# Pool adds up softmax numerators of three key tiles before TensorE sums them

## The chip, the cores and the metric

The kernel runs on one core of a Trainium2 chip. Its engines work side by side, each through its own queue of instructions in order: TensorE (PE in the profile; its weight loads are listed as PEld), VectorE (DVE), ScalarE (ACT), GpSimd (POOL) and SyncE (SP), whose queue here holds most of the DMA issues. An instruction starts when it is at the head of its engine's queue and when the semaphores that it waits for have come. The metric is the time of one execution on the device in microseconds (us); the time before is the median of three runs.

## The reference, cut to what matters

The reference is a decoder of two layers on an input of 4 batches x 512 tokens x 512 features, with layer norms behind each part: causal self-attention, cross-attention and a feed-forward part in layer 0; causal self-attention, a mixing of tokens by a thresholded similarity and a mixture of experts in layer 1. The change concerns the two self-attentions:

```python
    def _L0_attn_ref(hidden_states, Wq, bq, Wk, bk, Wv, bv, Wo, bo):
        HIDDEN = 512
        NUM_HEADS = 16
        ...
        scores = jnp.einsum('bhqd,bhkd->bhqk', q, k) * scale
        causal = jnp.tril(jnp.ones((S, S), dtype=bool))
        scores = jnp.where(causal, scores, jnp.float32(-jnp.inf))
        attn = jax.nn.softmax(scores, axis=-1)
        out = jnp.einsum('bhqk,bhkd->bhqd', attn, v)
```

and, because of tiles that share a buffer, the mixing part, whose thresholds depend only on the second input `ctx_512` and are worked out ahead, beside the self-attentions:

```python
    def _L1_xattn_ref(h, adj_raw, Wq, Wk, gamma_raw):
        ...
        sim = jnp.einsum('bhnd,bhmd->bnm', Q, K) / (jnp.sqrt(jnp.float32(d)) * H)
        k = max(1, int(n * TOP_K_RATIO))
        topk_vals = jax.lax.top_k(sim, k)[0]
        threshold = topk_vals[:, :, -1:]
```

## The kernel before, in words

The stages follow one another in time: self-attention of layer 0 (0 to 540 us), cross-attention (540 to about 1010), feed-forward (to 1414), self-attention of layer 1 (1414 to 1945), mixing and routing (to 2190), experts (to 2584).

**A self-attention** treats 16 groups `n`, each 4 heads of one batch (`n = 4 b + g`). Keys lie on the partitions and queries along the free dimension, so scores are held transposed. Per group there are four key tiles `kb` of 128 keys; by causality tile `kb` needs only the queries from 128 `kb` on, so its numerators `p0` to `p3` are 4 heads x 512, 384, 256 and 128 queries, float32. The steps of one group are: `maxima` (L228–249: scores with queries on partitions, DVE takes each query's greatest score), `parts` (L251–259: DVE splits the maxima into three bfloat16 parts), `least` (L261–269: PE transposes them, ACT copies the result to `nmT`), `softmax(n, kb)` (L273–296: PE computes the transposed scores with the negated maxima and the causal mask added, ACT takes the exponential in two instructions of two heads each, which makes `p0` to `p3`), `values` (L298–315) and `finish` (DVE: reciprocal and product).

`values(n)` runs two passes of matmuls over the same numerators: with weights `ones` it sums the numerators over the keys (into a PSUM tile of the `tp` pool), with weights `va` it makes the weighted values (into a tile of the `mm` pool). In both, each key tile and each head is one matmul, 16 per pass, and the profile shows every such float32 matmul as two records. After each pass ACT copies the result out (L311).

The order of the work is written out by hand: a loop over time steps `t` with `n, m = divmod(t, 4)` issues, at each step, `maxima(n, 3 - m)`; `least(n - 1)` at `m = 0`; `values(n - 2)` at `m = 1` or else a projection of the next batch; one `softmax` call of group `(t - 5) // 4`, with `kb` in the order 2, 1, 0, 3; then `finish`, `parts` and one step of a background generator. `in_order` (L416–429) chains PE's matmuls of the self-attention in that order. On the other engines a scheduler places the instructions; each engine keeps the order it got. The last batch of each layer has no next batch's projections beside it. PSUM pools in this stage: three pairs (`sc`), one `tp` buffer, one `mm` buffer.

**The background** of layer 0 is `split_context` (L435–461) followed by the threshold selection of batches 0 and 1; that of layer 1 is the selection of batches 2 and 3. `split_context` loads a 128 x 512 tile `ct` of the context per batch, scales it on Pool and splits it there into three bfloat16 parts `ct0`, `ct1`, `ct2`, which SP writes to DRAM (`ctx_part`); behind the four batches come 12 DMAs from `ctx_part` to `keys` and 16 from a tile of ones to `keys`, for the cross-attention. The selection loads the same context tile again (`scT`, L950–951, in `Similarities.tile`), makes two projections `sqk` and four similarity tiles `sim` with six matmuls per batch (L955, L960), each through the one `tp` buffer and a copy out, and then bisects for the threshold (L992–1010): in each step ACT takes signs with a running count (L998, into the tag `junk`, two buffers), and Pool updates `mid` with five small operations (L1006–1010). Two halves of two tiles take turns. At the end of a bisection ACT and DVE use a tile `y` (L1018–1021).

All tiles of the background come from one pool (`sims` in layer 0, `sims2` in layer 1) with one buffer per tag where nothing else is said: tiles of one tag share its buffers and wait for each other.

Of the kernel before, what the change touches and what calls it, by code (L numbers as in the profile page):

```python
# [13 lines left out]
F32 = mybir.dt.float32  # L14
BF16 = mybir.dt.bfloat16
U32 = mybir.dt.uint32
AF = mybir.ActivationFunctionType
ALU = mybir.AluOpType
# [3 lines left out]
P = 128  # L22
B, S, D = 4, 512, 512
NT = S // P
# [16 lines left out]
def decoder_kernel(ctx: ExitStack, tc: tile.TileContext, a: dict, out: bass.AP):  # L41
    nc = tc.nc
    V, A, G, T = nc.vector, nc.scalar, nc.gpsimd, nc.tensor
# [17 lines left out]
    def psum_tp(dt=F32, n=4):  # L61
        return ps["tp"].tile([P, n, P], dt, tag="tp", name="tp")

    def psum_mm():
        return ps["mm"].tile([P, 512], F32, tag="mm", name="mm")
# [10 lines left out]
    ones = const.tile([P, P], F32, tag="ones", name="ones")  # L76
# [59 lines left out]
    def self_attention(pre, first, background=lambda: None):  # L136
        HD, NG, NJ = 32, 4, 4
        scale = 1.0 / math.sqrt(HD)
        multiply, transpose = in_order()
        with tc.tile_pool(name=pre + "w", bufs=1) as wp, tc.tile_pool(  # L140
            name=pre + "qkv", bufs=2
# [126 lines left out]
                NM[n] = po.tile([P, S], BF16, tag="nmT", name="nmT")  # L268
                A.copy(NM[n], tp.rearrange("p i t -> p (i t)"))

            PR = {}

            def softmax(n, kb):  # L273

# [2 lines left out]
                m = S - kb * P  # L277
                p = PR[n, kb] = po.tile(
                    [P, NJ, m], F32, tag=f"p{kb}", name=f"p{kb}", bufs=2 if kb == 2 else 1
# [14 lines left out]
                for h in range(NJ // 2):  # L294
                    heads = p[:, 2 * h : 2 * h + 2, :]
                    A.activation(heads, sc[h][:, :, :m], AF.Exp)  # L296

            def values(n):  # L298

                b, g = divmod(n, NG)  # L300
                o, t = psum_mm(), psum_tp().rearrange("p n t -> p (n t)")
                for to, left in ((t, None), (o, VA[b % 2])):
                    for kb in range(NT):
                        for j in range(NJ):
                            multiply(
                                to[HD * j : HD * (j + 1), kb * P :],
                                ones[:, :HD] if left is None else left[:, kb, NJ * g + j, :],
                                PR[n, kb][:, j, :], start=(kb == 0), stop=(kb == NT - 1),
                            )
                    u = po.tile([P, S], F32, tag="us" if left is None else "u", name="u", bufs=1)  # L310
                    A.copy(u, to)  # L311
                    if left is None:
                        sums = u
                        yield
                if g == 0:
                    O[b] = po.tile([P, NG, S], F32, tag="oT", name="oT", bufs=1)
                F[n] = sums, u
# [59 lines left out]
            for t in range(NT * total + 6):  # L377
                n, m = divmod(t, NT)
                k = t - 5
# [14 lines left out]
                if m == 1 and n > 1:  # L394
                    dense = values(n - 2)
                elif t >= 6:
                    dense = project(b, u // NT, "qkv"[u % NT]) if b < B and u % NT < 3 else iter(())
                else:
                    dense = begin(2)
# [35 lines left out]
    def split_context(pool):  # L435


        for b in range(B):
            ct = pool.tile([P, S], F32, tag="ct", name="ct")
            nc.sync.dma_start(ct, a["ctxT"][:, ts(b, S)])  # L440
            G.tensor_scalar(ct, ct, 0.25, None, ALU.mult)
            for k in range(3):
                c = pool.tile([P, S], BF16, tag=f"ct{k}", name=f"ct{k}")
                G.tensor_copy(c, ct)
                nc.sync.dma_start(ctx_parts[k][:, ts(b, S)], c)
                if k < 2:
                    G.tensor_tensor(ct, ct, c, ALU.subtract)
            yield
        for p, k in enumerate(KPART):
            nc.sync.dma_start(  # L450
                keys[0][ts(p, XD)], ctx_parts[k].rearrange("(g d) t -> d g t", d=XD)
            )
        one = pool.tile([P, S], BF16, tag="ct0", name="ct0")
        G.memset(one, 1.0)
        for r in range(P // 32):
            nc.sync.dma_start(
                keys[1][32 * r : 32 * r + XD], ctx_parts[2].rearrange("(g d) t -> d g t", d=XD)
            )
            for b in range(B):
                nc.sync.dma_start(  # L460
                    keys[1][32 * r + XD : 32 * (r + 1), :, ts(b, S)],
                    one[:XD].unsqueeze(1).to_broadcast([XD, XG, S]),
                )
        yield
# [472 lines left out]
    class Similarities:  # L937
# [8 lines left out]
        def tile(self, b, i, tag="sim"):  # L946

            if self.b != b:
                self.b = b
                cT = self.pool.tile([P, S], F32, tag="scT", name="scT")  # L950
                nc.sync.dma_start(cT, a["ctxT"][:, ts(b, S)])
                self.qk = []
                for k in range(2):
                    ps = psum_tp().rearrange("p n t -> p (n t)")
                    T.matmul(ps, self.w[k], cT, start=True, stop=True)  # L955
                    t = self.pool.tile([P, S], F32, tag=f"sqk{k}", name=f"sqk{k}")
                    V.tensor_copy(t, ps)
                    self.qk.append(t)
            ps = psum_tp().rearrange("p n t -> p (n t)")
            T.matmul(ps, self.qk[0][:, ts(i, P)], self.qk[1], start=True, stop=True)  # L960
            s = self.pool.tile([P, S], F32, tag=tag, name=tag)
            A.activation(s, ps, AF.Copy, scale=float(np.float32(1.0 / (math.sqrt(32.0) * 4))))
            return s
# [432 lines left out]
    with tc.tile_pool(name="sims", bufs=1) as mp:  # L1396
        selection, background = selecting((0, 1), mp, split_context(mp))
        with psum(3, 1, 1):
            self_attention("L0", True, background)
            for _ in selection:  # L1400
                pass
# [17 lines left out]
    with tc.tile_pool(name="sims2", bufs=1) as mp:  # L1419
        selection, background = selecting((2, 3), mp)  # L1420
        with psum(3, 1, 1):
            self_attention("L1", False, background)
            for _ in selection:
                pass
# [49 lines left out]
```

## Time and profile before

| what | value |
|---|---|
| runs | 2602.18, 2584.24, 2590.51 us; median 2590.51 us |
| profiled execution | 2586.26 us; span of its core 2584.5 us |
| mean granted PE clock | 0.956 |
| PE busy, 0–540 us / 1414–1945 us | 484.17 of 540 / 483.29 of 531 us |
| ACT busy, same stretches | 208.50 / 220.53 us |
| DVE busy, same stretches | 269.23 / 265.57 us |
| POOL busy, same stretches | 100.72 / 70.01 us |
| granted PE clock, same stretches | 0.97 / 0.95 |
| first block of `sums` records, 512 columns (by shape) | 256 records, 35.6 us |
| 384, 256, 128 columns | 27.0, 19.9, 13.0 us |

Line 1 of the page gives each engine's busy time and its share of the span. The slices cut the span into 40 equal parts of 64.6 us; each digit is a busy share in tenths. A row of the groups names source line, engine, operation, the tiles written and read, partitions x elements, and the count; behind the first bar stand total busy time and mean duration in ns, behind the second the idle time of the engine just before, and what ended it. The timeline lists start, duration, engine, line and tiles; an engine with a trailing q is its queue of DMA issues, and a bracket gives the idle time before and what ended it. PE's records overlap since matmuls are pipelined, so the length of a pass is read from the start of the first matmul to the start of the work behind it.

### The profile page before, as it was taken

What the parts mean: (1) busy time and instruction counts of PE and PEld (TensorE: products, weight loads), DVE (VectorE), ACT (ScalarE), POOL (GpSimd) and SP (SyncE); (2) the same over time, 40 slices, a digit from 0 to 9 for tenths busy, and PEclk for the clock granted to TensorE, in tenths of its full rate; (3) what the DMA queues carried; (4) which work ended last, traced back from release to release, by engine and by line L of the source; (5) the groups of instructions that cost most, each with busy time, mean ns of one, the idle gap of its engine ahead of it and who ended that gap; (6) DMA issues with size and microseconds to landing.
All of it is one profiled execution on the core that took longest, in us unless ns stands there. A gap on an engine that the chain in (4) does not pass through costs nothing. (4 is left out here: it accounts for less than half of the span.)

```text
span 2584.5 us, 34904 instructions
## 1 busy us (share of the span) xinstructions
PE 2284.4 (88%) x13080; PEld 1010.3 (39%) x13080; DVE 1437.7 (56%) x3146; ACT 1128.1 (44%) x1770; POOL 624.9 (24%) x1218
## 2 busy tenths in 40 slices
PE   6899999979899899998995899989985999999995
PEld 2334333423333333355553334434342334444442
DVE  2455455567878788578886355545554672111117
ACT  0632462326777677656663443282331430221211
POOL 7300120033334233066674310040000004000004
PEclk9999999889999999999998999989987999999997
DMA  6500000072412210000001100000001006534535
GB/s 217 149 22 1 1 1 1 1 265 94 130 34 91 74 34 17 1 1 1 1 1 32 52 1 1 1 1 1 1 3 58 9 1 231 164 106 157 173 118 183
DMA packets 89884, 156.93 MB, mean 61 GB/s; under 512 B 7152, under 2 KB 39280, under 8 KB 89712
## 3 DMA queue, kind: packets, MB, share of 16 engines
q1 hardware_dynamic: 72304, 115.86, 13.9%
q10 hardware_dynamic: 12288, 22.03, 2.3%
q0 software_dynamic: 5120, 16.78, 2.0%
q8 instruction: 103, 1.69, 0.3%
q14 instruction: 69, 0.57, 0.1%
HBM read 161.99 MB, written 47.71 MB: 81 GB/s over the span
## 5 line engine op out<-in xcount | busy, mean ns | idle before, releaser
L552 DVE TENSOR_REDUCE nm<-sc 128x2 f32<-128x1024 f32 x256 | 304.2, 1218 | 99.7 <-PE sc L422 99.1
L590 ACT ACTIVATE p<-sc 128x1024 f32<-128x1024 f32 x256 | 248.5, 1024 | 135.3 <-PE sc L422 135.3
L246 DVE CUSTOM_DVE_ANT_0 e<-sc,late_keys 128x256 bf16<-128x256 f32 (+3 forms) x512 | 222.8, 484 | 130.9 <-PE sc L422 130.7
L296 ACT ACTIVATE p<-sc 128x512 f32<-128x512 f32 (+3 forms) x256 | 165.9, 700 | 234.1 <-PE sc L422 233.9
L422 PE MATMUL mm<-p,va 128*32 128x512 f32 (+3 forms) x2048 | 217.4, 529 | 0.4 <-ACT oT L605 0.3
L1339 PE MATMUL sc<-wug,xbT 128*128 128x512 f32 x384 | 185.9, 600 | 12.8 <-issue 7.0
L422 PE MATMUL sc<-qs,ks 128*128 128x512 bf16 x512 | 149.7, 384 | 29.3 <-DVE nm L552 28.1
L422 PE MATMUL sc<-ks,qs 128*128 128x512 bf16 x512 | 158.3, 394 | 1.8 <-DVE nm L552 1.6
L422 PE MATMUL sc<-kT,qT 32*128 32x512 f32 (+3 forms) x1024 | 128.8, 497 | 19.1 <-ACT p L296 15.7
L324 DVE RECIPROCAL u<-u 128x128 f32<-128x128 f32 x128 | 108.4, 909 | 64.6 <-ACT u L311 64.6
L422 PE MATMUL sc<-qT,kT 32*128 32x256 f32 (+3 forms) x1024 | 129.2, 504 | 14.4 <-DVE st L246 12.5
L998 ACT ACTIVATE junk<-sim,mid 128x512 bf16<-128x512 f32 x176 | 125.1, 724 | 16.3 <-POOL mid L991 16.3
L1366 POOL DMA_INDIRECT yg<-ys,pi x32 | 33.4, 1043 | 364.3 <-DMA ys<-yb 340.4
L743 POOL TENSOR_TENSOR y<-z 128x512 f32<-128x512 f32 (+1 forms) x48 | 97.4, 2041 | 87.3 <-DVE z L728 87.3
L1346 DVE TENSOR_TENSOR h<-sc,sl 128x256 f32<-128x256 f32 x48 | 20.2, 421 | 163.4 <-ACT sl L1344 163.4
L1339 PEld LDWEIGHTS sc<-wug,xbT 128*128 128x128 f32 x384 | 68.5, 192 | 82.4 <-issue 74.9
L743 POOL TENSOR_TENSOR z<-y 128x512 f32<-128x512 f32 x64 | 95.2, 1506 | 3.4 <-issue 2.1
L1353 PE MATMUL sc<-wd,hT 128*128 128x512 f32 x192 | 93.2, 609 | 0.0
L422 PEld LDWEIGHTS sc<-kT,qT 32*128 32x128 f32 x1024 | 49.7, 188 | 109.5 <-issue 74.1
L422 PEld LDWEIGHTS <-ks 128*128 128x128 bf16 x512 | 50.2, 99 | 108.1 <-issue 63.1
L1336 DVE COPY xbT<-tp 128x512 f32<-128x512 f32 x48 | 32.9, 685 | 104.6 <-PE tp L1334 104.6
L422 PEld LDWEIGHTS sc<-qT,kT 32*128 32x128 f32 x1024 | 50.4, 191 | 92.0 <-issue 62.0
(299 smaller groups left out, 4255.5 us busy)
## 6 DMA issues: line engine op xcount, KB each, us to landing
wug<-in_Wu SPq DMA_DIRECT2D x48, 512.0 KB
wug<-in_Wg SPq DMA_DIRECT2D x48, 512.0 KB
wd<-in_Wd SPq DMA_DIRECT2D x48, 512.0 KB
xs<-zero SPq DMA_DIRECT2D x3, 4096.0 KB
xb<-xs SPq DMA_DIRECT2D x48, 256.0 KB
ys<-yb ACTq DMA_DIRECT2D x48, 256.0 KB
w<-in_w_gate SPq DMA_DIRECT2D x16, 512.0 KB
w<-in_w_up SPq DMA_DIRECT2D x16, 512.0 KB
```

The costliest lines, as they stand in the source:

```text
L246: V.tensor_tensor_reduce(e, at[r], late_keys[:, (NT - m) * P :], 1.0, LOWEST, ALU.add, ALU.max, accum_out=st[:, i, r : r + 1],)
L296: A.activation(heads, sc[h][:, :, :m], AF.Exp)
L324: V.reciprocal(sums[:, ts(i, P)], sums[:, ts(i, P)])
L422: ins = op(*args, **kw)
L552: V.tensor_reduce(NM[n][:, i, 2 * h : 2 * h + 2], sc, AX.X, ALU.max, negate=True)
L590: A.activation(p[:, 2 * h : 2 * h + 2, :], sc[h], AF.Exp)
L743: then(pool, getattr(G, op)(*args))
L998: A.activation(e, s[k], AF.Sign, bias=bias[:, k : k + 1], accum_out=to[:, k : k + 1])
L1336: V.tensor_copy(xbT, tp)
L1339: T.matmul(pp[:, 0, :], xbT[:, c, :], wug[s][:, c, :, :].rearrange("p q f -> p (q f)"), start=(c == 0), stop=(c == NK - 1),)
L1353: T.matmul(pp[:, 1, :], hT[:, c, :], wd[s][:, c, :], start=(c == 0), stop=(c == F // P - 1),)
L1366: G.indirect_dma_start(out=y, out_offset=None, in_=ys, in_offset=bass.IndirectOffsetOnAxis(pos[k][:, t : t + 1], 0),)
```

## The change

In `softmax`, Pool adds the numerators that several key tiles have for the same later queries. A new tile `R[n]` (tag `r`, 4 heads x 384 queries, float32, one buffer) stands for queries 128 to 511. With `kb == 1`, `R`'s last 256 columns become `p1 + p2`; with `kb == 0`, its first 128 columns become `p1 + p0` and `p0` is added to its last 256. Each is done for two heads at a time, six Pool instructions per group. In `values`, the pass with `ones` now sums `p0`'s first 128 columns, `R` and `p3`, 12 matmuls in place of 16; the pass with `va` is as it was. The remaining edits are tags: `ct` and `scT` take the tag `y` (one buffer), `ct0` to `ct2` the tag `junk` (two buffers), where each had a buffer of its own.

```diff
-            PR = {}
+            PR, R = {}, {}
...
                     A.activation(heads, sc[h][:, :, :m], AF.Exp)
 
+                for h in range(NJ // 2):
+                    heads = slice(2 * h, 2 * h + 2)
+                    if kb == 1:
+                        if not h:
+                            R[n] = po.tile([P, NJ, S - P], F32, tag="r", name="r", bufs=1)
+                        G.tensor_tensor(
+                            R[n][:, heads, P:], p[:, heads, P:], PR[n, 2][:, heads, :], ALU.add
+                        )
+                    elif kb == 0:
+                        r = R[n][:, heads, :]
+                        G.tensor_tensor(
+                            r[:, :, :P], PR[n, 1][:, heads, :P], p[:, heads, P : 2 * P], ALU.add
+                        )
+                        G.tensor_tensor(r[:, :, P:], r[:, :, P:], p[:, heads, 2 * P :], ALU.add)
+
             def values(n):
...
                 for to, left in ((t, None), (o, VA[b % 2])):
-                    for kb in range(NT):
+
+                    if left is None:
+                        parts = [(PR[n, 0][:, :, :P], 0), (R.pop(n), 1), (PR[n, 3], 3)]
+                    else:
+                        parts = [(PR[n, kb], kb) for kb in range(NT)]
+                    for p, q in parts:
                         for j in range(NJ):
                             multiply(
-                                to[HD * j : HD * (j + 1), kb * P :],
-                                ones[:, :HD] if left is None else left[:, kb, NJ * g + j, :],
-                                PR[n, kb][:, j, :], start=(kb == 0), stop=(kb == NT - 1),
+                                to[HD * j : HD * (j + 1), q * P : q * P + p.shape[2]],
+                                ones[:, :HD] if left is None else left[:, q, NJ * g + j, :],
+                                p[:, j, :],
+                                start=q < (2 if left is None else 1),
+                                stop=q == NT - 1 or (left is None and q == 0),
                             )
...
-            ct = pool.tile([P, S], F32, tag="ct", name="ct")
+            ct = pool.tile([P, S], F32, tag="y", name="ct")
...
-                c = pool.tile([P, S], BF16, tag=f"ct{k}", name=f"ct{k}")
+                c = pool.tile([P, S], BF16, tag="junk", name=f"ct{k}", bufs=2)
...
-        one = pool.tile([P, S], BF16, tag="ct0", name="ct0")
+        one = pool.tile([P, S], BF16, tag="junk", name="ct0", bufs=2)
...
-                cT = self.pool.tile([P, S], F32, tag="scT", name="scT")
+                cT = self.pool.tile([P, S], F32, tag="y", name="scT")
```

## The prediction

> **What bounds the kernel now.** I read the page's busy line and its slices first.
>
> ```profile
> PE 2284.4 (88%) x13080; PEld 1010.3 (39%) x13080; DVE 1437.7 (56%) x3146; ACT 1128.1 (44%) x1770; POOL 624.9 (24%) x1218
> ...
> PE   6899999979899899998995899989985999999995
> ...
> POOL 7300120033334233066674310040000004000004
> ```
>
> TensorE (PE) is busy 88% of the span and Pool 24%; in the slices of the two self-attentions (0–540 us, 1414–1945 us) PE shows 9s where Pool shows 0 to 3. The averages hide stages with different limits, so next the busy times of single stretches (columns: window, length, busy and count of PE, PEld, DVE, ACT, POOL, granted clock, DMA share, GB/s):
>
> ```profile
> 195.00:260.00 65.00, 64.88 (x429) 27.28 (x428) 34.69 (x111) 18.40 (x28) 0.00 (x0) 1.00 0.00 1
> 1615.00:1680.00 65.00, 64.54 (x426) 26.77 (x423) 36.80 (x109) 19.11 (x29) 0.24 (x2) 1.00 0.00 1
> 82.00:141.00 59.00, 50.55 (x309) 19.94 (x308) 29.13 (x91) 49.55 (x122) 23.52 (x125) 0.91 0.33 79
> 1679.00:1743.00 64.00, 52.18 (x352) 21.64 (x348) 29.73 (x80) 51.78 (x128) 28.98 (x132) 0.89 0.00 1
> 540.00:544.00 4.00, 1.04 (x8) 0.88 (x9) 1.96 (x4) 0.61 (x1) 4.00 (x9) 0.51 1.04 327
> 544.00:548.00 4.00, 3.30 (x14) 1.54 (x14) 1.59 (x2) 1.41 (x2) 3.29 (x9) 0.50 1.06 405
> 548.00:552.00 4.00, 3.93 (x26) 2.22 (x24) 4.00 (x4) 1.11 (x2) 3.08 (x8) 0.71 1.05 410
> ```
>
> Rows 1 and 2: in the plain stretches PE never waits and Pool is free, so work taken off PE is time saved. Rows 3 and 4, beside the selection of batches 0 and 3: ScalarE (ACT) is the busier engine for its part, 49.55 of 59 and 51.78 of 64 us; PE waits some 15% there. Rows 5 to 7: after PE stood still (7.5 us from 534 to 542) its granted clock is 0.51, 0.50, then 0.71. Idle time of PE costs more than itself.
>
> **Part 1: fewer columns in the sums.** The timeline of one group in a plain stretch, and of the last two groups of L0 (columns: start, duration, what, count):
>
> ```profile
> 221.66 2.36 PE L422 MATMUL tp<-p,ones 128*32 128x512 f32 x32
> 223.95 0.71 PE L422 MATMUL sc<-qT,kT 32*128 32x256 f32 x8
> 241.37 1.94 ACT L296 ACTIVATE p<-sc 128x1024 f32<-128x1024 f32 x2 [3.43 <-PE sc L422]
> ...
> 498.92 1.94 ACT L296 ACTIVATE p<-sc 128x1024 f32<-128x1024 f32 x2 [2.98 <-PE sc L422]
> 501.38 2.36 PE L422 MATMUL tp<-p,ones 128*32 128x512 f32 x32 [0.52 <-ACT nmT L269]
> 510.98 2.60 ACT L296 ACTIVATE p<-sc 128x1024 f32<-128x1024 f32 x4 [1.01 <-PE sc L422]
> 512.86 2.35 PE L422 MATMUL tp<-p,ones 128*32 128x512 f32 x30
> ```
>
> The sums pass holds PE from 221.66 to 223.95, 2.29 us for 512+384+256+128 = 1280 columns per head. After the change it has 128+384+128 = 640. By columns that is 1.15 us; small blocks cost more than their share (0.22–0.27 us for 128 columns against 0.86 for 512), so I take 1.2–1.25 left and a gain of 1.05 us (0.9 to 1.15). There are 32 groups, 16 per layer; 28 of them are dense: 28 × 1.05 = **−29.4** (−25 to −32).
>
> **Part 2: Pool's adds.** Per group two of 2x256 elements per partition (for `kb`=1), then two of 2x128 and two of 2x256 (for `kb`=0): 192 instructions. The groups that price them (mean ns after the bar's first number):
>
> ```profile
> L193 POOL TENSOR_TENSOR x<-x,L0bo 128x512 f32<-128x512 f32 x16 | 19.7, 1265 | 0.0
> L618 POOL TENSOR_TENSOR x<-oc,x 128x256 f32<-128x256 f32 x32 | 26.2, 820 | 108.5 <-DVE oc L614 108.5
> ```
>
> So 2 × 1.265 = 2.5 us for `kb`=1 and 2 × (0.82+1.265) = 4.2 us for `kb`=0; from the first half's exponential to a finished `R` 3.9 to 4.6 us, since the second half follows without a gap. In the dense group above the first half ends at 242.34, `R` at about 247; the next sums pass of that group stands at some 250.7. The cover is 3.7 us of other matmuls: cost nothing. If it were gone, each group would lose what `R` is late.
>
> Cover is missing in the last two groups of each layer, with no projections left. n=14: exponentials from 498.92 (half ends about 499.9), `R` at 503.9–504.5, sums at 501.38 now; the 128 columns of `p0` run meanwhile, 384 and 128 columns (0.64 + 0.25) behind `R`, so it ends at 504.8–505.4 where it ends at 503.7 now: +1.1 to +1.7. n=15: half ends 512.0, `R` 516–516.6, sums end 516.9–517.5 where they end at 515.2 now: +1.7 to +2.3. Two layers: **+6.5** (5.6 to 8).
>
> What DVE pays: at 54.03 a DVE instruction with two SBUF operands, `rest` (L255), took 1.18 us beside Pool's L193 adds, at 205.00 alone 0.18; the PSUM-fed maxima don't stretch. `parts` has four such, up to 3 us later, needed some 4 us after: 0 (bound +3). The Trainium skill ("GPSIMD Engine Reference", Engine selection) speaks against putting a two-input elementwise operation on GpSimd, about twice as slow as VectorE. Rows here agree (1.265 us, against 0.69 for 512-wide DVE operations at L325), and by that rule the adds on DVE would shorten `R`'s chain by half, at most the 6.5 of the tail.
>
> **Part 3: the tags, at the beginning of L0.** `ct2` now shares two buffers with `ct0` and `ct1`, and `scT` shares one with `ct`. So batch 0's `scT` load (L951), issued at 27.51, can't start before the last `ct` is dead, and in SP's queue it now stands behind all the split's DMAs. In the order of instructions on each engine it goes from position 13 to 54, where the third `xt` load stands now. And PE's six similarity matmuls of batch 0 stand in a row behind `maxima(1,3)`, ahead of `least(1)`. The queue and PE now:
>
> ```profile
> 27.51 0.45 SPq L951 DMA_DIRECT2D scT<-in_ctxT  x1
> 65.23 6.00 SPq L450 DMA_DIRECT2D keys<-ctx_part  x8
> ...
> 97.64 0.61 SPq L181 DMA_DIRECT2D xt<-in_xT  x1
> ...
> 66.79 1.02 PE L955 MATMUL tp<-scT,swq 128*128 128x512 f32 x2
> 96.01 0.40 PE L422 MATMUL tp<-ident,pm 128*128 128x128 bf16 x4
> ```
>
> PE reaches that place at about 96.0 − 6.3 (the similarity matmuls and their waits, no longer before it) − 2.0 (an exponential's wait that goes) = 88. The load can be issued at 97.64 at the earliest; the keys' transfers drain at about 100.3, so its 256 KB land at about 101.5; the split itself is later by δ: each `ct2` cast waits for `ct0`'s write (about 3 us), and the next `ct` for it, hence δ = 4.6 (1 to 8). The load lands at 106, PE stands 18 us (14 to 22). The order in PE's queue is fixed, so the ready scores and values of group 0 stand behind it. Then six matmuls with one PSUM buffer go in turn with their copies: 1.8 us each by 66.79 to 68.54, 10.8 against 5.7 now, +5 (4 to 6). Then the clock: +4 (0 to 8) by the rows at 540–552, half speed for some 8 us. **+27** (18 to 36). The Trainium skill ("TensorE: Matmul & The Clock Gate", Part 1) has full speed back after about 3.4 us of sustained work; by it the clock would cost at most 2. The rows at 544–552, busy 3.30 and 3.93 of 4 us and still at 0.50 and 0.71, say longer.
>
> In L1 and for later loads `scT` is wanted over 100 us after its buffer is free: nothing.
>
> **Part 4: Pool's adds in the selection.** A bisection step is ACT's signs, then five small Pool operations of 0.2 us (1.2 us for the chain), then the next signs; two halves alternate, so one half's two signs (1.45 us) cover the other's Pool work. In the changed order about eight blocks of adds (2.5 or 4.2 us) stand among these steps. Each holds ACT for 1.05 or 2.75 us, about 15 in all, and exponentials and `nmT` copies stand behind the signs. Half of it reaching PE: **+8**; nothing if ACT catches up, 20 if all does and the clock falls with it.
>
> **Sum.** −29.4 + 6.5 + 27 + 8 = +12. The profiled execution took 2586.26 us (span 2584.5, 1.8 around it): **2598**. That execution lies 4 under the median, 2590.51, so by the median it would be 2602. All good bounds: −32+6+18 = −8; all bad: −25+8+3+36+20 = +42.
>
> **Rivals.**
> - B: the load isn't late at PE, because PE gets there later than 88 or the load is issued past the keys' DMAs. Only the serial chain stays: −29.4+6.5+5+8 = −10: 2576 (2566 to 2582). For it: nothing but the shared buffer orders the load. Against: position 54 in SP's queue.
> - C, slower: Pool in the selection. Where a block of adds outlasts the 1.45 us of the other half's signs, ACT waits, PE waits behind its exponentials, and the clock falls: eight blocks lose their whole 3.35 us, 27, and some 5 at low clock in place of +8: 2622 (2613 to 2633). It decides as soon as PE has no ready matmuls ahead. For it: ACT at 81–84% in those stretches. Against: PE is already waiting there for the same signs.
> - D: the change doesn't do what it says: the sums are half as wide, but `R` is late in dense groups too (Pool's strided reads slower than L193's, over 8 us a group), so only 8 of the 29 stay: 2619.
>
> **Chances.** Forecast 0.64 (own range 2580 to 2616), B 0.14, C 0.13, D 0.09. The range leaves out half of B and half of C with the ends: 2575 to 2625. 1% of the time is 25.9 us, about what a measurement of this kernel can tell from no change. Faster by more (below 2560.4): 0.05, B with a cheaper selection. Slower by more (above 2612.1): C and D most of the time, 0.17, and the forecast's tail, 0.06: 0.23. The rest 0.72.
>
> **What would show it.** Part 1: sums passes of about 1.2 us in the plain stretches, PE still at 64 of 65 there. Part 2: four groups whose sums wait for Pool. Part 3: a hole in PE near 88–106 ended by the `scT` load, six similarity matmuls at 1.8 us pitch after it, a clock near 0.5 behind. Part 4: waits of ACT's signs for `mid` that are longer than now, with adds before `mid` on Pool. The prediction is wrong if PE has no such hole, if `R` is late in dense groups, or if PE's hole hides selection work that it would else have waited for.

## The result, and the profile after

The changed kernel takes 2604.13 us (median of 7 runs, 2598.89 to 2610.20); the kernel before 2590.51 us in the same comparison. The ratio is 1.0052, 95% interval 1.0032 to 1.0071: 14 us slower, a little outside the measurement's uncertainty. Forecast was 2598 us on the base of the profiled execution, 2602 on that of the median, range 2575 to 2625. The profiled execution took 2601.68 us, its span is 2600.0, 15.5 more than before.

The page's busy line and slices of the changed kernel:

```profile
PE 2269.2 (87%) x12824; PEld 1001.5 (39%) x12824; DVE 1443.9 (56%) x3146; ACT 1129.7 (43%) x1770; POOL 828.0 (32%) x1410
...
PE   7689989878989899989987789989985999999995
...
POOL 6241242142333333147676243152230004000004
```

PE has 256 records fewer (two for each of the 128 matmuls), Pool 192 more and 203 us more work. PE's busy time falls by only 15 us, though half of the sums' columns are gone, and the second slice, from 65.0 us on, shows a 6 where an 8 stood.

The timeline shows why (columns: start, duration, engine, line, tiles, count; in brackets PE's idle time before and what ended it). First the beginning of layer 0, then a group in a plain stretch, then the last two groups of layer 0:

```profile
87.12 1.14 PE L444 MATMUL sc<-kT,qT 32*128 32x512 f32 x8
100.89 1.43 SPq L973 DMA_DIRECT2D scT<-in_ctxT  x1
105.75 2.08 PE L977 MATMUL tp<-scT,swq 128*128 128x512 f32 x2 [17.49 <-DMA scT<-in_ctxT]
108.61 2.08 PE L977 MATMUL tp<-scT,swk 128*128 128x512 f32 x2 [0.78 <-DVE sqk L979]
111.47 2.08 PE L982 MATMUL tp<-sqk,sqk 128*128 128x512 f32 x2 [0.78 <-DVE sqk L979]
...
119.75 2.07 PE L982 MATMUL tp<-sqk,sqk 128*128 128x512 f32 x2 [0.69 <-ACT sim L984]
122.51 0.58 PE L444 MATMUL tp<-ident,pm 128*128 128x128 bf16 x4 [0.69 <-ACT sim L984]
...
249.00 0.42 PE L444 MATMUL tp<-p,ones 128*32 128x128 f32 x8
249.24 0.83 PE L444 MATMUL tp<-r,ones 128*32 128x384 f32 x8
249.88 0.40 PE L444 MATMUL tp<-p,ones 128*32 128x128 f32 x8
250.22 1.00 PE L444 MATMUL sc<-qT,kT 32*128 32x256 f32 x6
...
525.35 1.49 PE L444 MATMUL tp<-r,ones 128*32 128x384 f32 x4 [0.15 <-POOL r L311]
527.25 0.85 PE L444 MATMUL tp<-r,ones 128*32 128x384 f32 x2 [0.41 <-POOL r L311]
...
540.71 0.84 PE L444 MATMUL tp<-r,ones 128*32 128x384 f32 x4 [0.70 <-POOL r L311]
542.62 0.52 PE L444 MATMUL tp<-r,ones 128*32 128x384 f32 x2 [1.06 <-POOL r L311]
```

PE ends `maxima(1,3)` at 88.26, waits 17.49 us for the `scT` load, which SP issues at 100.89 behind the last `keys` DMA, and then goes through six links of 2.8 us each. A plain group's sums last from 249.00 to 250.22, 1.22 us in place of 2.29, and no wait for `R` stands there. In the last two groups PE does wait for `R`: 2.3 us in those of layer 0 and 2.2 us in those of layer 1.

The granted clock, in the windows view (us, PE, PEld, DVE, ACT, POOL, clock, DMA share, GB/s):

```profile
90.00:100.00 10.00, 0.00 (x0) 0.00 (x0) 0.83 (x4) 0.00 (x0) 0.30 (x1) 0.57 0.88 181
100.00:110.00 10.00, 3.47 (x4) 1.00 (x4) 0.69 (x1) 0.00 (x0) 0.00 (x0) 0.50 0.74 191
110.00:120.00 10.00, 7.16 (x8) 1.75 (x8) 3.52 (x6) 2.09 (x4) 0.94 (x5) 0.50 0.00 0
120.00:130.00 10.00, 9.31 (x50) 3.78 (x54) 3.33 (x6) 7.60 (x21) 3.93 (x22) 0.72 0.00 0
215.00:280.00 65.00, 64.88 (x457) 27.75 (x460) 38.67 (x114) 19.60 (x30) 12.70 (x12) 1.00 0.05 17
```

The clock is down to 0.57 in the hole and at 0.50 through the chain of six. In the plain stretch PE is busy 64.88 of 65 us, as before, with Pool now at 12.7.

Pool's adds by shape (the mean in ns behind the comma):

```profile
L311 POOL TENSOR_TENSOR r<-r,p 128x512 f32<-128x512 f32 x64 | 81.2, 1270 | 0.0
L303 POOL TENSOR_TENSOR r<-p,p 128x512 f32<-128x512 f32 x64 | 80.0, 1271 | 367.0 <-ACT p L296 367.0
...
L308 POOL TENSOR_TENSOR r<-p,p 128x256 f32<-128x256 f32 x64 | 46.5, 727 | 99.1 <-ACT p L296 99.1
```

1.27 and 0.73 us, where 1.265 and 0.82 were taken from other lines.

**A ledger by groups.** The start of each group's value pass (`mm<-p,va`), in the timeline of a run minus that of the kernel before, tells where time is lost or gained. Changes over a stretch of groups, in us. The other columns are kernels of the experiments below: "again" is a second execution of the changed kernel, "best" and "best, DVE" are from the third set.

```
stretch                 changed   again  tags alone  tags+adds  short sums   best  best, DVE
L0, groups 0-1           +28.4    +30.5      +28.2      +29.5       +0.3      +3.4     +1.1
L0, groups 2-7            -4.8     -4.4       +4.1       +2.5       -5.9      -5.9     -5.1
L0, groups 8-13           +1.0     -1.6       +3.0       +3.2       -3.0      -1.3     -1.9
L0, groups 14-15          +3.3     +3.4       +1.7       +1.7       -3.5      +1.8     -0.1
from there to L1, 0        0.0     -3.2       -4.9       -4.8       -5.9      -3.8     -2.5
L1, groups 1-6            -5.6     -5.6        0.0        0.0       -5.5      -5.5     -2.6
L1, groups 7-13          -10.5     -9.0        0.0       +0.1      -10.9      -7.7     -8.9
L1, groups 14-15          +2.9     +4.6        0.0       +3.6       -0.6       0.0     +1.3
```

In the plain groups of the changed kernel each step is −1.07 (the first group of a batch, −0.55). Each column is one execution. The row between the layers, where hardly any changed line runs, shows what such a column is uncertain by: 0 to −6 us here. The two executions of the changed kernel differ by 0 to 3 us a row and come to the same sum, 14.6 us.

### The profile page after: what moved, and what is told of

Its sections match the earlier page's. It is cut to its first block, busy times and chain, and to the rows that moved or that the text cites. A ratio compares the mean times of both kernels' runs of the same rounds, so it can differ in the third digit from the quotient of the medians.

```text
span 2600.0 us, 34609 instructions
## 1 busy us (share of the span) xinstructions
PE 2269.2 (87%) x12824; PEld 1001.5 (39%) x12824; DVE 1443.9 (56%) x3146; ACT 1129.7 (43%) x1770; POOL 828.0 (32%) x1410
## 5 line engine op out<-in xcount | busy, mean ns | idle before, releaser
L303 POOL TENSOR_TENSOR r<-p,p 128x512 f32<-128x512 f32 x64 | 80.0, 1271 | 367.0 <-ACT p L296 367.0
```

The source lines that it names most:

```text
L303: G.tensor_tensor(R[n][:, heads, P:], p[:, heads, P:], PR[n, 2][:, heads, :], ALU.add)
```

## The experiments

My theory A, from the prediction: a gain of 1.07 us wherever PE is the bound, a late `scT` load at the beginning of layer 0, late sums in the last two groups of each layer, and ScalarE held up by Pool in the selections. The rivals stand with each run. The first set was run where the kernel before itself took 2612.28 us, the second and third where it took 2590.31 and 2590.62; so runs are compared by their ratio to the kernel before of their own set, and what was expected in us is read as a ratio to 2590.5.

### First set: the parts apart

**Tags alone.** The kernel before with nothing but

```diff
-            ct = pool.tile([P, S], F32, tag="ct", name="ct")
+            ct = pool.tile([P, S], F32, tag="y", name="ct")
-                c = pool.tile([P, S], BF16, tag=f"ct{k}", name=f"ct{k}")
+                c = pool.tile([P, S], BF16, tag="junk", name=f"ct{k}", bufs=2)
-        one = pool.tile([P, S], BF16, tag="ct0", name="ct0")
+        one = pool.tile([P, S], BF16, tag="junk", name="ct0", bufs=2)
-                cT = self.pool.tile([P, S], F32, tag="scT", name="scT")
+                cT = self.pool.tile([P, S], F32, tag="y", name="scT")
```

> The kernel before with the four tag edits alone: no adds on Pool, sums pass of 1280 columns per head. Theory A (the shared buffer of scT makes PE stand still at the beginning of layer 0): a hole in PE of about 17 us near 88 to 106 us, six similarity matmuls in a row behind it, and 28 us more than before: 2618 us (2611 to 2624). Rival U (the tags are nearly free, the loss is Pool's adds): 2590 to 2596 us.

Measured: 2639.09 us, 1.0113 (1.0094 to 1.0131), 29 us slower. Its timeline has the hole and the slow links:

```profile
107.10 2.08 PE L955 MATMUL tp<-scT,swq 128*128 128x512 f32 x2 [19.15 <-DMA scT<-in_ctxT]
109.96 2.07 PE L955 MATMUL tp<-scT,swk 128*128 128x512 f32 x2 [0.78 <-DVE sqk L957]
```

The tags alone cost more than the whole change does. Rival U is out.

**Short sums alone.**

```diff
+                    if left is None:
+                        parts = [(PR[n, 0][:, :, :P], 0), (None, 1), (PR[n, 3], 3)]
+                    else:
+                        parts = [(PR[n, kb], kb) for kb in range(NT)]
...
+                            if p is None:
+                                multiply(
+                                    to[HD * j : HD * (j + 1), P:], ones[:, :HD],
+                                    ones.unsqueeze(1).to_broadcast([P, NT - 1, P]),
+                                    start=True, stop=False,
+                                )
+                                continue
```

> The kernel before with a sums pass of 640 columns per head and no adds on Pool: the 384-column block is read from a constant tile of ones, so the sums of later queries are not the true ones. Tags as before. Theory A (PE is the bound wherever it has no wait): each of the 32 groups saves 1.07 us, 34 us in all: 2556 us (2551 to 2561). Rival D (the end of the sums pass is not what the next work waits for): less than half of that, 2574 us or more.

Measured: 2577.21 us, 0.9875 (0.9855 to 0.9894). That is 33 us in 32 groups, 1.02 each. As a ratio theory A expected 0.985 to 0.989 and rival D 0.9936 or more (2577.21 us lies above D's 2574 only because this set's base is longer). D is out: the sums' columns are on the path that sets the end.

**Adds without a reader.**

```diff
-                    if left is None:
+                    if left is None and False:
                         parts = [(PR[n, 0][:, :, :P], 0), (R.pop(n), 1), (PR[n, 3], 3)]
```

(and the same condition in `start` and `stop`).

> The changed kernel with its tags and its adds on Pool, but the sums pass of 1280 columns as before, so R is made and not read. Against the run with the tags alone this prices Pool's adds where nobody waits for R. Theory A: the adds cost only what they hold ScalarE up during the two layers' selections, 4 to 10 us: 2622 to 2628 us. Rival V (the adds slow VectorE or PE in the plain stretches too, half a us per group or more): 2634 us or more. Rival W (the adds cost nothing): 2618 us.

Measured: 2641.35 us, 1.0115 (1.0095 to 1.0136), against 1.0113 for the tags alone. The intervals are some 5 us to either side: no cost of the adds is seen, though the lower end of my 4 to 10 us is not excluded; V's 16 us are, and W is nearest. The ledger has the two runs alike, within 1.7 us a row, but for the last two groups of layer 1, where the adds go with 3.6 us although nobody reads `R`. PE waits no longer there than with the tags alone, but the granted clock is lower (the first row is the run with the adds, the second the tags alone, each from the value pass of group 13 to that of 14):

```profile
1943.00:1960.00 17.00, 15.55 (x149) 7.28 (x148) 8.36 (x26) 6.83 (x11) 6.36 (x6) 0.80 0.00 1
1943.00:1958.00 15.00, 12.61 (x149) 6.20 (x147) 7.24 (x26) 6.75 (x11) 0.00 (x0) 1.00 0.01 1
```

**`scT` on its own tag again.**

```diff
-                cT = self.pool.tile([P, S], F32, tag="y", name="scT")
+                cT = self.pool.tile([P, S], F32, tag="scT", name="scT")
...
-        st = small.tile([P, NT, 6], F32, tag="bst", name="bst")
+        st = small.tile([P, NT, 6], F32, tag="bst", name="bst", bufs=2)
```

(the second in both places that use it).

> The changed kernel with scT on a tag of its own again; the space comes from two buffers in place of four for the layer norm's statistics. Pool's adds and the short sums pass stay. Theory A: no hole in PE at 88 us, the similarity matmuls spread among the others again, 28 us less than the changed kernel: 2576 us (2569 to 2583). Rival U: within 5 us of the changed kernel, 2600 to 2608 us.

Measured: 2601.03 us where the kernel before took 2612.28: 0.9957 (0.9944 to 0.9970), faster than before. Expected was a ratio of 2576 to 2590.5, 0.9944. So of all the tag edits it is the one buffer of `scT` that costs: 0.0097 of the time (1.0054 for the changed kernel in the second set, less 0.9957), 25 us. The difference is taken across two sets; two more such differences, of the kernels of the third set from their counterparts in the second, are 24 and 28 us.

### Second set: clock, tail, engine

**The changed kernel again**, as the reference of this set.

> The changed kernel as it is, so that the other runs of this set have it on the same chip: 1.005 of the kernel before (1.003 to 1.007).

Measured: 2604.92 us, 1.0054 (1.0035 to 1.0074).

**PE kept busy in the hole.** In `least`, ahead of the transposes:

```diff
+                if first and n == 1:
+                    idle = psum_pair()
+                    for _ in range(18):
+                        multiply(idle[:, 0, :], ones, w["q"][:, 0, :], start=True, stop=True)
                 tp = psum_tp(BF16)
```

> The changed kernel with 18 matmuls of 512 columns on constant weights, whose result nobody reads, put in PE's queue ahead of the six late similarity matmuls, so that PE is not idle while the scT load is awaited. The load and the chain of six stay. Theory A (the idle time lowers the granted clock for as long again as the hole): the clock stays near 1.0, the six links take 1.8 us instead of 2.8, and the stretch behind them is at full speed: 9 us less than the changed kernel (6 to 12). Rival K (the clock comes back within a few us of work, so it costs little): 0 to 3 us less.

Measured: 2605.77 us, 1.0050 (1.0030 to 1.0070): nothing. But the timeline and the windows of this run say that the test wasn't the one I meant:

```profile
86.84 15.72 PE L448 MATMUL sc<-L0wq,ones 128*128 128x512 f32 x36
105.89 2.08 PE L981 MATMUL tp<-scT,swq 128*128 128x512 f32 x2 [3.33 <-DMA scT<-in_ctxT]
108.75 2.08 PE L981 MATMUL tp<-scT,swk 128*128 128x512 f32 x2 [0.78 <-DVE sqk L983]
```

```profile
90.00:100.00 10.00, 10.00 (x25) 4.50 (x24) 0.00 (x0) 0.00 (x0) 0.00 (x0) 1.00 0.87 172
100.00:110.00 10.00, 5.89 (x10) 1.78 (x9) 0.69 (x1) 0.00 (x0) 0.00 (x0) 0.79 0.75 194
110.00:120.00 10.00, 7.16 (x8) 1.61 (x7) 3.38 (x6) 1.95 (x4) 0.94 (x5) 0.50 0.00 2
```

The clock was 1.00 through the former hole. The 18 matmuls ended too early, 3.33 us of waiting were left, and the links run at 2.8 us with the clock at 0.50, just as behind 17.49 us. So rival K, whose time this is, isn't confirmed either: the clock did not come back within the chain. Either a wait of 3.3 us is enough, or the gaps within the chain lower the clock; the third set separates these.

**The last two groups of each layer summed as before.**

```diff
-                for h in range(NJ // 2):
+                for h in range(NJ // 2 if n < B * NG - 2 else 0):
...
-                    if left is None:
+                    if left is None and n < B * NG - 2:
```

(and in `start` and `stop`).

> The changed kernel, but the last two groups of each layer sum their four key tiles on PE as before and have no adds on Pool. Theory A (in these four groups R comes after PE has reached the sums): PE waits for no R any more, and value passes that were 6.2 us later in the four groups together are not: 6 us less than the changed kernel (4 to 8). Rival T (the four groups are late for another reason, such as ScalarE's exponentials): within 2 us of the changed kernel.

Measured: 2595.74 us, 1.0017 (1.0003 to 1.0031), 9 us less than the changed kernel. Rival T is out as an account of the whole. The size is somewhat above what was expected; the ledger has 6.2 us for the four groups of the changed kernel (3.3 + 2.9) and 8.0 in its second execution. But in this run, without an add there, group 14 of layer 0 is still 1.8 us later than in the kernel before. PE waits for no `R`; the granted clock is 0.72, against 0.90 in the same stretch before:

```profile
515.00:533.00 18.00, 16.67 (x148) 8.08 (x148) 6.43 (x25) 6.75 (x11) 0.00 (x0) 0.72 0.00 1
```

**The adds on VectorE**: the three `G.tensor_tensor` of `softmax` become `V.tensor_tensor`.

> The changed kernel with the six adds of each group on VectorE in place of Pool. Theory A (VectorE has no room in its order: each add stands ahead of maxima and waits for an exponential there): PE waits for score buffers in the plain groups, 0.5 to 1.5 us in each of 32 groups: 15 to 45 us more than the changed kernel. Rival S (the Trainium skill, GPSIMD Engine Reference, Engine selection: a two-input elementwise operation is about twice as fast on VectorE): R is ready 2 us earlier in the four last groups and nothing else moves: 4 to 7 us less than the changed kernel.

Measured: 2592.35 us, 1.0002 (0.9989 to 1.0014), 13 us less than the changed kernel. My theory was wrong by its sign. Rival S had the sign, and less than the size: by the ledger 6 of the 13 us lie in the last two groups of each layer (6.2 in the changed kernel, 0.2 here), the rest in rows that vary by some 3 us between two executions of one kernel. VectorE's adds by shape:

```profile
L311 DVE TENSOR_TENSOR r<-r,p 128x512 f32<-128x512 f32 x64 | 43.8, 684 | 0.0
L303 DVE TENSOR_TENSOR r<-p,p 128x512 f32<-128x512 f32 x64 | 43.7, 690 | 55.7 <-ACT p L296 55.6
L308 DVE TENSOR_TENSOR r<-p,p 128x256 f32<-128x256 f32 x64 | 27.0, 422 | 79.9 <-ACT p L296 79.9
```

0.69 us against Pool's 1.27: 1.85 times as fast. The Trainium skill ("GPSIMD Engine Reference", Engine selection) puts GpSimd at about twice VectorE's time for such an operation; these rows agree. In the plain groups the step is −0.81 or −1.07 in place of −1.07, so VectorE's order does cost a little there; in the last two groups of layer 0 it is +0.98 and −0.79 in place of +1.69 and +1.58.

### Third set: what adds up

**Own tag and VectorE.**

> The changed kernel with scT on a tag of its own and the adds on VectorE. If the two gains add up (1.0054 of the kernel before for the changed kernel, 0.0097 less by the own tag, 0.0052 less by VectorE): 0.990 to 0.992 of the kernel before. If VectorE's gain was only a cover of the late start of layer 0, it is not there a second time: 0.995 to 0.997, as with the own tag alone.

Measured: 2568.04 us, 0.9908 (0.9891 to 0.9924).

**Own tag, Pool, and the last two groups as before.**

> The changed kernel with scT on a tag of its own, the adds on Pool, and the last two groups of each layer summed as before. If these two add up (0.0097 and 0.0037 less than the changed kernel): 0.992 of the kernel before (0.990 to 0.994). Against the same with VectorE this also shows whether Pool's adds cost anything outside these four groups: if they hold ScalarE up in the selections, as the prediction had it, this kernel is some 4 to 8 us behind the one with VectorE; if not, within 2 us of it.

Measured: 2568.45 us, 0.9910 (0.9894 to 0.9927). Both are 22 us faster than the kernel before, and faster than it and the changed kernel by more than the intervals. The two come to the same time within 0.4 us. That does not show that Pool's adds cost nothing outside the last groups, as I had meant it to: the run with VectorE keeps the adds in the last groups, so the two differ in more than the engine. By the ledger VectorE is 3.7 us behind in the plain rows (0.8 + 2.9), and Pool 4.1 us behind in the three rows with selections (2.3 + 0.6 + 1.2), each uncertain by some 3 us. A cost of Pool's adds in the selections of some 4 us would be hidden in this comparison.

**22 extra matmuls in place of 18.**

> As the run with 18 extra matmuls, but with 22, so that PE is busy until the scT load has landed and no wait of 3.3 us is left in front of the six links. Theory A2 (what lowers the clock is a wait of some 3 us, however short the hole otherwise): the links go at 1.8 us and the end is 5 to 9 us earlier than the changed kernel. Rival G (the gaps of 0.7 to 0.8 us in the chain of six lower the clock themselves): the links stay at 2.8 us or fall back to it after one or two, and the end is within 3 us of the changed kernel.

Measured: 2598.73 us, 1.0032 (1.0019 to 1.0044), 6 us less than the changed kernel by the ratios; the intervals overlap, but the timeline is plain:

```profile
87.81 19.15 PE L448 MATMUL sc<-L0wq,ones 128*128 128x512 f32 x44
106.80 1.02 PE L981 MATMUL tp<-scT,swq 128*128 128x512 f32 x2
108.60 1.13 PE L981 MATMUL tp<-scT,swk 128*128 128x512 f32 x2 [0.78 <-DVE sqk L983]
```

```profile
110.00:120.00 10.00, 6.40 (x16) 2.13 (x16) 5.57 (x9) 4.38 (x9) 2.43 (x14) 1.00 0.01 4
120.00:130.00 10.00, 8.93 (x105) 4.03 (x104) 3.79 (x11) 10.00 (x28) 5.32 (x29) 1.00 0.01 2
```

The same gaps of 0.78 us stand in the chain and the clock stays at 1.00; the links take 1.8 us. The first value pass starts 18.9 us later than before, where the changed kernel has 24.8 (27.4 in its second execution). Rival G is out: the gaps alone didn't lower the clock here; with a wait of 3.33 us ahead of them, or one of 17.49, it was at 0.50.

## Why the prediction came out, point by point

**The total: near, and in part by luck.** Forecast was +12 on the profiled execution, measured +15.4 there and +14 in the medians. The +8 of the selection is not seen in any run, and VectorE's share, put at nothing, was something; a dearer start and the stretches beside the selections made up for it. The prediction also took 1% for the least that can be told from no change; the interval here is some 0.2% to either side.

**The sums (−29.4): right.** 1.22 us are left of a pass (1.2 to 1.25 forecast); plain groups step by −1.07; short sums alone give 1.02 per group.

**The last two groups (+6.5): right in size, in mechanism only in part.** The ledger has +6.2 (8.0 in the second execution), the run without adds there 9 us. PE waits for `R`, by name, for 4.5 us in the four groups. Two things stand beside them that the term didn't have: waits for VectorE's `pm` (below, 1.6 us), and a granted clock that is lower in these groups in several runs, also where PE waits for no `R` (0.72 with the old sums in layer 0, 0.80 with adds that nobody reads in layer 1). How the loss divides between waits and clock is not shown.

**The beginning (+27): right in mechanism and sum, with one term mis-sized.** The hole was to be 18 us at 88 to 106 and is 17.49 at 88.26 to 105.75. The chain of six was to take 10.8 us and takes 16.8 (105.75 to 122.51), since all of it runs at the half clock; clock and chain were counted as +4 and +5. By the 22-matmul run the clock's part is about 6. The "at most 2" that the prediction worked out from a page was a wrong use of it. The Trainium skill ("TensorE: Matmul & The Clock Gate", Part 1) has the full clock come back after some 3.4 us of sustained work; a chain that waits 0.7 to 0.8 us in each link of 2.8 was not such work here, as the clock of 0.50 through all of it shows. The runs price the whole at 25 us (own tag) to 29 us (tags alone).

**Pool in the selection (+8): not seen.** Adds without a reader showed no cost against tags alone, within some 5 us. (Pool against VectorE in the third set can't tell, as said there.) The waits of ScalarE's signs for the updates of the bisection's `mid`, in the changed kernel (us in total, times, longest):

```profile
ACT junk L1020 <- POOL mid L1032: 3.0, 4, 1.2
ACT junk L1020 <- POOL mid L1035: 2.3, 2, 1.6
```

The kernel before has no such waits. These are 5.3 us in six waits where 15 us in eight blocks were reckoned, so the term was mis-sized at its first step already, and "Half of it reaching PE" is not borne out. That the total still fits has a reason elsewhere: the start was dearer than its 27 (groups 0 and 1 lose 28.4 with their own gain of 2.1 already taken off), and the stretch around the second selection of layer 0 (groups 8 to 13) came out 1.0 later where −1.07 a group would be −6.4, or 1.6 earlier in the second execution. Neither the tags nor the adds are needed for that: with the short sums alone the stretch gains 3.0 and not 6.4. Groups 7 to 13 of layer 1 gain 10.5 where 7.5 were due, and 10.9 with the short sums alone, nothing with the tags alone; so that gain comes with the shorter sums. Why the one stretch gives less than its columns and the other more is not settled: no run isolates it.

**The rivals.** B (no hole) fell at the timeline. C's eight blocks on Pool are not seen, and its 2613 to 2633 us were not reached. D (`R` late in dense groups too) fell at the timeline: the plain groups step by −1.07 with no wait for `R`, and all such waits lie in the last two groups of a layer. (The D of the short sums, that the sums' columns don't set the end, is another one; it fell there.)

**What VectorE pays (0): wrong.** `rest` (L255) took 0.185 us in the median before and after, at most 1.18 and 1.17, and so looks unchanged. The sums say otherwise. `parts` by line, two lines before and then the same two after:

```profile
L254 DVE TENSOR_SCALAR pm<-st 128x16 bf16<-128x16 f32 x32 | 7.1, 222 | 1.0
L255 DVE SCALAR_TENSOR_TENSOR rest<-st,pm 128x16 f32<-128x16 f32 x32 | 6.9, 216 | 1.1
...
L254 DVE TENSOR_SCALAR pm<-st 128x16 bf16<-128x16 f32 x32 | 12.3, 383 | 1.1
L255 DVE SCALAR_TENSOR_TENSOR rest<-st,pm 128x16 f32<-128x16 f32 x32 | 12.3, 384 | 1.1
```

Of the 128 instructions of `parts` (four lines, 32 groups) 5 took over 0.3 us before and 18 in the changed kernel, 14 of these beside Pool's add of L303. In all the runs it is 13 to 18 where Pool has the adds and 3 to 6 where it has none; 3 with the adds on VectorE. In the plain groups this shows no cost: the step is −1.07. Ahead of the sums of group 14 PE has no other work and waits for the late `pm`, 0.80 us in layer 0 and 0.81 in layer 1 (in layer 0 alone in the second execution). In layer 0:

```profile
519.95 2.48 POOL L303 TENSOR_TENSOR r<-p,p 128x512 f32<-128x512 f32 x2 [11.90 <-ACT p L296]
521.31 1.17 DVE L255 SCALAR_TENSOR_TENSOR rest<-st,pm 128x16 f32<-128x16 f32 x1
523.04 0.40 PE L444 MATMUL tp<-ident,pm 128*128 128x128 bf16 x4 [0.80 <-DVE pm L259]
```

The prediction's "needed some 4 us after" holds for the dense groups and not for the last ones; in the kernel before the same matmul has no wait.

## What to carry to other kernels

An edit that only makes room can cost more than the main edit brings: here the shared buffer cost 25 us where the rest of the change brought 11 (0.9957). It moved a load from the 13th to the 54th place of its queue, and PE, whose order was fixed, stood behind it. Look up what each shared tag makes wait, in the order of the instructions on the queue, before the arithmetic of the main edit. Moving work to an idle engine showed no cost here where other work covers its chain, and did in the last rounds of a pipeline, where nothing is left to cover it; leave it out there. And look at what the moved work does to the small instructions of other engines beside it, by the sum of their times and not by the median.

## What the runs showed of the hardware

- A wait of 3.33 us ahead of a chain with gaps cost the same clock as one of 17.49 us: the links run at 2.8 us in both, at 1.8 us with no such wait. In these three runs what mattered is whether PE came into the chain at full clock.
- From half clock the chain did not get out while it lasted, though PE was busy 7.16 of 10 us in it; entered at full clock, it kept 1.00 at 6.40 of 10 us.
- 512-wide float32 adds took 1.27 us on Pool and 0.69 us on VectorE. The best kernel with either came to the same time (0.9910 with Pool's adds left out of the uncovered groups, 0.9908 with VectorE's in all).
- Beside Pool's adds small VectorE instructions (16 columns, 0.185 to 0.204 us in the median) took up to 1.17 us (L255) and 1.31 us (L254); in the changed kernel 14 of 128 took over 0.3 us beside the add of L303. With the adds on VectorE 3 of 128 took that long.
